# One stage of a two-layer image kernel put under a list scheduler: attention, spectral filters and weight preparation in the order of a table

## The chip, the cores and the metric

The kernel runs on one core of one Trainium2 chip. The core has a matrix engine (TensorE, PE in the profile, whose weight loads are the row PEld), a vector engine (VectorE, DVE), an activation engine (ScalarE, ACT), a general engine (GpSimd, POOL), and a queue engine (SyncE, SP) that here does nothing but issue DMAs. Each engine runs its own instructions strictly in the order in which they were written, and waits on semaphores for the others. The metric is the device time of the whole kernel in microseconds.

## The reference

The input is a batch of 16 images of 128 channels and 32 x 32 pixels, all in float32. Two "metaformer" layers are applied; each adds a token mixer and then a second mixer to the image.

```python
# layer 0: linear attention on channels, then a spectral filter over the pixels
x = x + conv0(ln_c(x))        # group norm, q/k/v, softmax(q), softmax(k), context = k v, out = context q, w_out
t = to_tokens(x)
t = t + ffn0(ln_t(t))         # sum over 16 filters: causal long convolution, then a 128x128 matrix each; 3 short taps
# layer 1: two 3x3 convolutions with a residual, then a mixture of 64 experts
x = x + conv1(ln_c(x))
t = to_tokens(x)
t = t + ffn1(ln_t(t))         # 8 best pixels per expert are gathered, gelu(x w1) w2, added back
```

`ln_c` and `ln_t` normalize each pixel over its 128 channels. The long convolution runs over 1024 channel vectors in a transform of the pixels: a sample is multiplied with cosine and sine tables (by "classes" of every eighth pixel), the spectrum is multiplied with the transform of the filters, and the result is turned back.

## The kernel before, in words

**Stages.** The kernel works through the batch in four stages, one after the other. (1) Attention of each sample, its second normalization, the three short taps, and its transform into a spectrum that is written to DRAM (lines 221 to 774). In the same stage the filters are transformed ("filters", lines 649 to 690), their matrices are mixed from four sets (into the tile `mst`, 16 steps), and the convolution weights and the inverse tables of layer 1 are prepared ("prepare", lines 692 to 735, on POOL). (2) The spectra are multiplied with the filters (lines 777 to 921). (3) Inverse transform, layer-1 convolutions and gating, sample by sample. (4) The experts and the final sum. The change touches stage 1 alone.

**One sample in stage 1** is the class `Attention`, with a method per step; a step issues one or a few instructions on one engine. In the order of the data: `tokens` (PE transposes the image by blocks of 128 pixels into a PSUM tile `big`), `moments` (DVE, four BATCH_NORM_STATS2 on that tile, line 135) and `tokens_copy` (ACT, the same tile to SBUF, line 376); `variance`, `root`, `scales` (line 127 to 129 and 390), `norm` (ACT, eight instructions, line 144); `spread`, `group`, `group_var`, `group_root`, `group_scale`; `channels` and `channels_copy` (back to channels first, line 424); `k`, `q` (PE, lines 451 and 433); maxima, exponents and sums on DVE and ACT; `k_scale` (POOL, line 476); `q_tokens`, `q_copy`, `context` (PE, line 499), `fold`, `fold2`, `out` (PE, line 534), `out_add` (DVE, line 539). Then the second half: `input` (PE, line 157), `moments2` (DVE, line 135), `input_copy` (ACT, line 550, the same PSUM tile), `scales2`, `norm2`; `even` and `odd` (PE, line 571), whose results pass ACT, DVE (`even_sums`, line 254; `odd_sums`) and POOL (`even_turns`, lines 287 to 293; `odd_turns` 1 to 4, lines 295 to 309) and go out to DRAM (`vd`, line 628); `taps_in`, `taps_copy`, `taps` (PE, line 639), `taps_add` (DVE, line 646) and a store of the image (`xd`, line 647).

**The order around the change.** PE, DVE, ACT and POOL are pinned to the order in which the program issues the steps; SP is not pinned in stage 1. The order before is a fixed period written by hand: a tuple `period` (line 742) names each step once with a distance `d`, and the loop runs it for `p` from -6 to 15 and calls each step for sample `p + d` (lines 760 to 771). So up to seven samples are in work, each step once per round; one step of the filters and one of the preparation is called per round. The first round that has a sample in all steps comes after six rounds, and the last six rounds run without new samples. `keep` (line 159) puts matmuls with no use between the steps at four places, from the table `idle` (line 354).

**Loads.** Two images are loaded ahead, then the tables `wf` and `phi` (1 MB each, lines 737 and 739); every `tokens` step loads the image two samples on (line 368). A step of the filters loads 512 KB of `mi` (line 683), and its use follows in the next round.

**The planner** `planned` (line 1783) is already in the kernel and orders stage 3. It takes a table (name, engine, microseconds, due date, what the step waits for, which tiles it opens and which it closes), a number of buffers for each tile, and a period. It keeps a clock for each engine and picks, among the steps that can start within 0.25 us of the earliest, the one with the smallest due date (due + sample x period):

```python
    hop, window, never = 0.09, 0.25, 1e18
    late = dict(PE=0.165, DVE=0.083, ACT=0.096, POOL=0.04, SP=2.0)
...
        soon = min(starts.values()) + window
        k = min((k for k, t in starts.items() if t <= soon), key=lambda k: (ops[k][2], starts[k]))
```

A step marked `DVEs`, and every POOL step, also takes a shared resource called "port", so that the two kinds are not planned at the same time. `late` is what passes from the end of a step to the moment when its result can be used; `SP=2.0` with 1.28 us for the transfer makes 3.28 us for a 512 KB load. The order that comes out is what the engines follow; the planner's clock is not kept at run time.

Of the kernel before, what the change touches and what calls it, by code (L numbers as in the profile page):

```python
# [69 lines left out]
def metaformer_kernel(ctx: ExitStack, tc: tile.TileContext, io: dict, out: bass.AP):  # L70
# [106 lines left out]
    with ExitStack() as l0:  # L177
# [43 lines left out]
        with ExitStack() as a0:  # L221
            aconst = a0.enter_context(tc.tile_pool(name="aconst", bufs=1))
            setup = a0.enter_context(tc.tile_pool(name="setup", bufs=2))
            work = a0.enter_context(tc.tile_pool(name="awork", bufs=2))


            spool = a0.enter_context(tc.tile_pool(name="spool", bufs=2))
            xpool = a0.enter_context(tc.tile_pool(name="xpool", bufs=8))
            ppool = a0.enter_context(tc.tile_pool(name="ppool", bufs=1))
            ps = a0.enter_context(tc.tile_pool(name="aps", bufs=2, space=PSUM))  # L230
# [120 lines left out]
            def small(shape, name):  # L351
                return work.tile(shape, F32, name=name, tag=name, bufs=5)

            idle = {("tokens", 1): 5, ("filters", 0): 4, ("channels", 0): 1, ("k", 1): 2}

            class Attention:
# [10 lines left out]
                def tokens(self):  # L367
                    if self.b + 2 < B:
                        load(self.b + 2)
# [4 lines left out]
                def tokens_copy(self):  # L374
                    self.tok = work.tile([P, NT, C], F32, name="tok", tag="tok", bufs=3)
                    nc.scalar.copy(self.tok, self.pt)
# [171 lines left out]
                def input_copy(self):  # L548
                    self.ub = work.tile([P, NT, C], F32, name="ub", tag="ub")
                    nc.scalar.copy(self.ub, self.pt)  # L550
# [74 lines left out]
                def odd_turns4(self):  # L625
                    butterflies(self.ao, self.xf, 1, self.sd)
                    for cs in (slice(0, 1), slice(1, NCH)) if self.b + 1 == B else (slice(NCH),):
# [21 lines left out]
            def filters():  # L649

                wfm = setup.tile([P, NQ // 2, 2 * P], F32, name="wfm", tag="mi")
                nc.vector.tensor_scalar(wfm, wf[:, 1::2, :], -1.0, None, ALU.mult)

                def values(q, dst):
                    for sgn in range(2):
                        w = wfm[:, q // 2, :] if sgn and q % 2 else wf[:, q, :]
# [4 lines left out]
                yield  # L661
                xf = spectrum_tile()
                for parity in range(2):
                    pe = class_values(parity, values)
                    t = class_copy(pe, 1)
                    ts = class_copy(pe, ROT) if parity else t
                    ab = class_sums(parity, pe, t)
                    class_differences(parity, ab, pe, ts)
                    yield
                    for part in range(2):  # L670
                        butterflies(ab, xf, parity, part)
                    if parity:
# [1263 lines left out]
```

## Time and profile before

| what | value |
|---|---|
| median of three runs | 1228.67 us (1227.26 to 1231.8) |
| the profiled execution | 1229.05 us, of which its span is 1227.0 us |
| mean granted TensorE clock | 0.988 |
| PE busy over the span | 94% |
| DVE, ACT, POOL busy | 76%, 59%, 49% |
| stage 1 | from the start to about 384 us (first matmul of stage 2 at 384.08) |
| first multiplication with the spectra | 397.91 us |

The chain of work that ended last says which engine's work the end of the kernel waited for, piece by piece. A row of a timeline gives start, length, engine, line and tile, and in brackets how long the engine had been idle before it and what released it. A busy PE is an overlapping count of pipelined matmuls: the time from one matmul group's start to the next is the better measure of its length. A window row gives the busy time of PE, PEld, DVE, ACT and POOL in a stretch, with counts, then the granted clock and the DMA share and rate.

### The profile page before, as it was taken

Reading aid. Unit: us, or ns where it says so; the run is one execution under the profiler, and the core shown is the slowest. Engines: PE = TensorE matmul, PEld = TensorE weight load, DVE = VectorE, ACT = ScalarE, POOL = GpSimd, SP = SyncE. Lnnn points to the kernel's source line nnn. Section 1 sums busy time; section 2 is a strip of 40 time slices with the busy share of each in tenths; the row PEclk is TensorE's granted clock in tenths of the full one; section 3 lists DMA queues with packets and bytes.
Section 4 is the critical chain, followed back from the end, with each engine's and each line's share of the span. In section 5 each row is a group of like instructions: output and inputs, shape, how many; then the busy total and the mean of one; then the engine's idle time right before and its main releaser. Section 6 shows DMA issues by size and latency. Waiting matters only on the chain.

```text
span 1227.0 us, 34351 instructions
## 1 busy us (share of the span) xinstructions
PE 1155.2 (94%) x14364; PEld 946.8 (77%) x14364; DVE 932.7 (76%) x1956; ACT 721.2 (59%) x1414; POOL 602.2 (49%) x800
## 2 busy tenths in 40 slices
PE   6889999999999999999997999999999999998996
PEld 4677767777677899998996888888888888885453
DVE  5888888887767677777764689898888989877335
ACT  4777777776656777877760445555555555554211
POOL 2436454664568788888882433343333333230003
PEclk9999999999999999999998999999999999999998
DMA  7004435243446244344348511233233322416998
GB/s 283 24 31 158 133 99 173 87 160 124 132 142 182 81 141 139 137 139 140 125 147 282 134 52 52 87 103 120 80 121 112 103 86 70 155 35 237 357 404 341
DMA packets 91243, 175.14 MB, mean 143 GB/s; under 512 B 5968, under 2 KB 42064, under 8 KB 90448
## 3 DMA queue, kind: packets, MB, share of 16 engines
q1 hardware_dynamic: 90448, 170.46, 41.1%
q0 software_dynamic: 640, 2.49, 0.6%
q8 instruction: 113, 1.85, 0.6%
q14 instruction: 42, 0.34, 0.1%
HBM read 110.28 MB, written 62.65 MB: 141 GB/s over the span
## 4 chain that ended last, share of the span: by engine, by line
PE 52%; DVE 22%; issue 10%; ACT 5%; DMA 5%; POOL 5%; SPq 0%; POOLq 0%; DVEq 0%; ACTq 0%
PE pcv L1013 10%; PE py L841 8%; PE pg L817 8%; PE big L639 6%; DVE bst L135 4%; PE big L172 3%; PE big L152 3%; PE big L571 3%; PE big L451 2%; PE big L534 2%; PE big L433 2%; DVE abss L1256 1%; DVE xp L1278 1%; DVE xp L1140 1%; POOL v L808 1%
## 5 line engine op out<-in xcount | busy, mean ns | idle before, releaser
L1013 PE MATMUL pcv<-v,cw 128*128 128x256 f32 x1152 | 258.2, 380 | 1.6 <-POOL v L1203 1.6
L1013 PEld LDWEIGHTS pcv<-v,cw 128*128 128x128 f32 x1152 | 214.7, 190 | 34.7 <-issue 4.9
L828 DVE COPY g<-pg 128x512 f32<-128x512 f32 x196 | 127.6, 682 | 67.9 <-PE pg L817 67.9
L830 ACT COPY g<-pg 128x512 f32<-128x512 f32 x316 | 161.1, 606 | 28.7 <-PE pg L817 27.9
L817 PE MATMUL pg<-ph,mst 32*128 32x128 f32 x4096 | 138.9, 278 | 1.4 <-DVE x L646 0.9
L817 PEld LDWEIGHTS pg<-ph,mst 32*128 32x128 f32 x4096 | 125.9, 187 | 15.6 <-DVE g L828 8.3
L841 PE MATMUL py<-g,v 128*32 128x128 f32 x4096 | 126.0, 276 | 1.9 <-POOL v L809 1.6
L841 PEld LDWEIGHTS py<-g,v 128*32 128x32 f32 x4096 | 109.2, 110 | 9.7 <-POOL v L809 2.1
L144 ACT ACTIVATE tok<-tok,sts 128x128 f32<-128x128 f32 x256 | 101.9, 480 | 16.9 <-DVE sts L1090 13.6
L135 DVE BATCH_NORM_STATS2 bst<-big 128x6 f32<-128x256 f32 x252 | 89.6, 416 | 19.9 <-PE big L152 10.7
L808 POOL TENSOR_TENSOR v<-xc 128x256 f32<-128x256 f32 x128 | 98.0, 790 | 9.9 <-DMA xc<-vd 9.2
L639 PE MATMUL big<-u,mu 128*128 128x128 f32 (+4 forms) x384 | 86.0, 380 | 0.0
L1203 POOL TENSOR_TENSOR v<-abss 128x256 f32<-128x256 f32 x64 | 49.1, 787 | 68.2 <-DVE abss L1199 56.8
L287 POOL TENSOR_TENSOR xf<-ab 128x256 f32<-128x256 f32 x34 | 24.8, 728 | 112.6 <-DVE ab L254 112.5
L1222 POOL TENSOR_TENSOR yo<-abss 128x256 f32<-128x256 f32 x32 | 23.5, 734 | 107.5 <-DVE abss L1218 107.5
L639 PEld LDWEIGHTS big<-u,mu 128*128 128x128 f32 x384 | 56.7, 191 | 18.0 <-issue 15.4
L571 PE MATMUL big<-wf,ub 128*128 128x256 f32 x256 | 63.5, 392 | 0.2
L809 POOL TENSOR_SCALAR v<-v 128x256 f32<-128x256 f32 x64 | 55.0, 860 | 5.6
L476 POOL TENSOR_TENSOR ke<-ke,ks 128x1024 f32<-128x1024 f32 x16 | 30.6, 1913 | 54.9 <-DVE qs L484 43.2
L144 ACT ACTIVATE tt<-tt,sts 128x128 f32<-128x128 f32 x120 | 47.8, 481 | 13.9 <-DVE sts L1090 13.9
L571 PEld LDWEIGHTS big<-wf,ub 128*128 128x128 f32 x256 | 47.0, 193 | 9.1 <-ACT xn L424 3.0
L915 ACT COPY yt<-py 128x512 f32<-128x512 f32 x60 | 35.1, 585 | 31.2 <-ACT g L830 17.6
(277 smaller groups left out, 2479.8 us busy)
## 6 DMA issues: line engine op xcount, KB each, us to landing
we<-in_weight SPq DMA_DIRECT2D x32, 1024.0 KB, 9.1
xc<-vd SPq DMA_DIRECT2D x64, 256.0 KB, 3.0
yd<-ys SPq DMA_DIRECT2D x32, 512.0 KB, 3.6
vd<-xf SPq DMA_DIRECT2D x15, 1024.0 KB, 5.1
y<-yd SPq DMA_DIRECT2D x15, 896.0 KB, 6.1
x<-in_x SPq DMA_DIRECT2D x16, 512.0 KB, 5.5
mi<-in_M_phi SPq DMA_DIRECT2D x16, 512.0 KB, 4.7
xd<-x SPq DMA_DIRECT2D x16, 512.0 KB, 6.2
```

What stands on the lines that cost most here:

```text
L135: nc.vector.bn_stats(bst[:, j : j + 2, :].rearrange("p j s -> p (j s)"), src[:, j : j + 2, :].rearrange("p j c -> p c j"),)
L144: nc.scalar.activation(dst[:, j, :], src[:, j, :], AF.Identity, bias=nm[:, j : j + 1], scale=r[:, j : j + 1],)
L571: nc.tensor.matmul(dst, self.ub[:, q, :], wf[:, q, :], start=True, stop=True)
L639: nc.tensor.matmul(self.pa[:, a:hi], mu[:, NF - 1 - si, tap, :], self.u[:, a - tap : hi - tap], start=(tap == 0), stop=(tap == KU - 1),)
L808: nc.gpsimd.tensor_tensor(vv[:, x, 1:, bs], e, o, op)
L809: nc.gpsimd.tensor_scalar(v[:, :, 0, bs], v[:, :, 2, bs], -1.0, None, ALU.mult)
L817: nc.tensor.matmul(pg[r][:, i], mst[rs, 4 * q + i, :], ph[rs, c, :], start=True, stop=True,)
L828: nc.vector.tensor_copy(dst, src)
L830: nc.scalar.copy(dst, src)
L841: nc.tensor.matmul(py[rows, x, kl, :], v[:, (x * NM + m) * JL + jl, 1 - ri : 3 - ri, :] .rearrange("p k b -> p (k b)"), g[:, ((x * 2 + ri) ...
L1013: nc.tensor.matmul(pc[:, i], wt[:, dy, k, :], v[:, k, dy * WT : dy * WT + HT], start=(dy == 0), stop=(dy == 2),)
L1203: nc.gpsimd.tensor_tensor(v[:, k, WT : WT + HT], self.ab[:, 0], self.ab[:, 1], op)
```

## The change

**Order.** The tuple `period` is replaced by a table in the planner's form, with one row per step of a sample, and rows `f_...` for the filters and `p_...` for the preparation, which exist once. `planned` is called with a period of 520.01, and the loop runs its order. The generator `filters` becomes a class `Filters` with a method per step. Some yields of `prepare` move, so that a step is shorter.

**Loads.** The load of an image is no longer part of `tokens`. Eight images are loaded ahead, interleaved with `wf` and `phi`; the other eight are steps of the table, which need one of eight buffers, freed by the store of an earlier image. The write of a spectrum is a step (`spec`) of its own, and `mi` loads (`f_ld0` to `f_ld15`) and uses (`f_m0` to `f_m15`) are separate steps. A load of `prepare` is issued in a step of 0.02 us (`p_0`, `p_9`, `p_18`, `p_22`), and its first use is the step after.

**Copies.** `tokens_copy` and `input_copy` become two instructions of half a tile, which is one PSUM bank each; the table lets them start 0.7 us before the end of the statistics.

**Pools.** The pools of stage 1 get `reuse_waits="tile"`, as those of stage 3 have. The small tiles get 7 buffers for 5. The useless matmuls stand at other places: 12 calls as before.

```diff
-            setup = a0.enter_context(tc.tile_pool(name="setup", bufs=2))
-            work = a0.enter_context(tc.tile_pool(name="awork", bufs=2))
+            setup = a0.enter_context(tc.tile_pool(name="setup", bufs=2, reuse_waits="tile"))
+            work = a0.enter_context(tc.tile_pool(name="awork", bufs=2, reuse_waits="tile"))
...
-                return work.tile(shape, F32, name=name, tag=name, bufs=5)
+                return work.tile(shape, F32, name=name, tag=name, bufs=7)
-            idle = {("tokens", 1): 5, ("filters", 0): 4, ("channels", 0): 1, ("k", 1): 2}
+            idle = {("begin", 0): 4, ("tokens", 1): 2, ("tokens", 2): 2, ("group", 0): 2, ("channels", 0): 2}
...
                 def tokens(self):
-                    if self.b + 2 < B:
-                        load(self.b + 2)
...
-                    nc.scalar.copy(self.tok, self.pt)
+                    for h in range(2):
+                        js = slice(h * NT // 2, (h + 1) * NT // 2)
+                        nc.scalar.copy(self.tok[:, js], self.pt[:, js])
...
-                    nc.scalar.copy(self.ub, self.pt)
+                    for h in range(2):
+                        js = slice(h * NT // 2, (h + 1) * NT // 2)
+                        nc.scalar.copy(self.ub[:, js], self.pt[:, js])
...
                     butterflies(self.ao, self.xf, 1, self.sd)
+
+                def spec(self):
                     for cs in (slice(0, 1), slice(1, NCH)) if self.b + 1 == B else (slice(NCH),):
...
+            class Filters:
+                def fetch(self, k):
+                    m, i = divmod(k, NF)
+                    self.mi = getattr(self, "mi", {})
+                    self.mi[k] = setup.tile([P, MB, C], F32, name="mi", tag="mi")
+                    nc.sync.dma_start(self.mi[k], io["M_phi"][i, :, m * MB : (m + 1) * MB, :])
+
+                def mix(self, k):
+                    m, i = divmod(k, NF)
+                    es, mi = slice(m * MB, (m + 1) * MB), self.mi.pop(k)
...
+            for b in range(2, 4):
+                load(b)
             nc.sync.dma_start(wf, io["wf"])
+            for b in range(4, 6):
+                load(b)
             phi = spool.tile([P, NQ, 2, P], F32, name="phi", tag="xf")
             nc.sync.dma_start(phi, io["phi"])
+            for b in range(6, 8):
+                load(b)
-            period = (
-                ("q_max", 3), ("out_add", 1), ("tokens", 6), ("moments", 6), ("context", 2),
...
+            table = (
+                ("load", "SP", 1.28, 2153.3, "", "x", ""),
+                ("tokens", "PE", 0.88, 4110.1, "load", "big:t tok", ""),
+                ("moments", "DVE", 1.337, -1802.8, "tokens~.6", "", "big:t"),
+                ("tokens_copy", "ACT", 1.034, 110.7, "tokens moments~.7", "", "big:t"),
...
+                ("scales", "DVE", 0.747, -1588.3, "variance root", "", ""),
...
+                ("k_scale", "POOL", 1.87, -1214.9, "k_recip", "", ""),
...
+                ("input_copy", "ACT", 1.034, 2302.1, "input moments2~.7", "ub", "big:i"),
...
+                ("spec", "SP", 2.6, -1380.7, "odd_turns4 odd_turns2 odd_turns even_turns2", "", "xf"),
...
+                ("taps", "PE", 5.22, 6831.9, "taps_copy", "big:ta", "u"),
+                ("taps_add", "DVE", 1.147, 655, "taps input", "", "big:ta"),
+                ("store", "SP", 1.28, 6675.6, "taps_add input", "", "x"),
...
+                ("f_wfm", "DVE", 0.607, 3426.6, "", "mi:w", ""),
+                ("f_val0", "PE", 3.45, 3203.6, "f_wfm f_phi", "big:f0", ""),
...
+                ("f_ld1", "SP", 1.28, 3049.5, "f_ld0", "mi:1", ""),
+                ("f_m1", "DVEs", 1.187, 5750.1, "f_ld1 f_m0", "", "mi:1"),
...
+                ("p_9", "POOL", 0.02, 2845.1, "p_8", "", ""),
+                ("p_10", "POOL", 0.96, 2246.3, "p_9", "", ""),
...
+            )
+            buffers = dict(x=8, big=3, s=2, tok=3, xn=3, qe=2, ke=2, qt=2, cx=2, wy=2, wt=2, ub=2, et=2, er=1, ab0=2, ab1=2, xf=2, sd=2, u=2, mi=2)
+            START = {
...
+                "f_wfm": 14.5, "f_val0": 20.0, "f_ld0": 30.0, "p_0": 25.0,
+            }
...
+            order = planned(
+                table, buffers, B, 520.01, lambda b, name: b > 0 and name[:2] in ("f_", "p_"),
+                lambda b, name: START.get((b, name), START.get(name, 0.0)),
+            )
+            samples, setting, preparing = {}, Filters(), prepare()
             with tc.manual_schedule(engines=PINNED):
-                for p in range(-reach, B):
-                    next(preparing, None)
-                    for name, d in period:
-                        b = p + d
...
+                keep(ps, "s", idle["begin", 0])
+                for b, name in order:
+                    kind, _, rest = name.partition("_")
...
+                    elif kind == "p":
+                        next(preparing, None)
+                    elif name == "load":
+                        if b >= 8:
+                            load(b)
+                    elif name != "store":
...
+                        getattr(samples[b], "q_" if name == "q" else name)()
+                    keep(ps, "s", idle.get((name, b), 0))
```

## The prediction

> **What bounds the kernel now.** The change is confined to stage 1 (start to 384.08 us), so I read that stage first, by windows: one while the pipeline of samples fills, six steady rounds, and, since the same planner already orders stage 3, a steady part of stage 3. Columns: window, length, busy PE, PEld, DVE, ACT, POOL, clock, DMA share, GB/s.
>
> ```profile
> 60.00:80.00 20.00, 17.25 (x152) 13.76 (x151) 18.48 (x53) 15.39 (x32) 4.04 (x2) 0.91 0.06 21
> 125.18:253.14 127.96, 123.90 (x853) 94.80 (x853) 106.27 (x260) 95.47 (x199) 66.51 (x104) 1.00 0.41 130
> 700.00:1060.00 360.00, 348.97 (x2221) 307.32 (x2219) 320.08 (x641) 193.87 (x369) 139.44 (x183) 1.00 0.29 93
> ```
>
> In the steady part PE is busy 123.90 of 127.96 us: 20.65 us of work in a round of 21.33. That is the floor for a sample; DVE (17.7 us a round), ACT (15.9) and POOL (11.1) lie under it. While the pipeline fills, DVE is nearly full (18.48 of 20) and PE is not. Next, who makes PE wait in a steady round: PE's timeline, and the entry of line 550.
>
> ```profile
> 186.60 1.89 PE L571 MATMUL big<-wf,ub 128*128 128x256 f32 x8
> 189.16 1.09 PE L172 MATMUL big<-ident,ub 128*128 128x128 f32 x8 [0.66 <-ACT ub L550]
> ...
>   DVE bst L135: 33.3, 15
> ...
>   PE big L172: 9.9, 12
> ```
>
> There is one stall a round, 0.66 us: `taps_in` waits for the copy of line 550, and that copy for the statistics of line 135 on the same tile. Over the stage it costs PE 9.9 us: 2.3 in the first two rounds, 7.6 later. Third, the fill: DVE's and ACT's timelines (two of DVE's rows, ACT's root of sample 0 ahead of them), then DVE's first work on `k`.
>
> ```profile
> 12.30 0.21 ACT L122 ACTIVATE sts<-sts 128x8 f32<-128x8 f32 x1
> ...
> 20.43 0.69 DVE L254 TENSOR_TENSOR ab<-big,et 128x512 f32<-128x512 f32 x1 [3.05 <-ACT et L245]
> 21.63 0.31 DVE L127 TENSOR_TENSOR sts<-sts 128x8 f32<-128x8 f32 x1
> ...
> 31.31 1.22 DVE L460 TENSOR_REDUCE ks<-big 128x32 f32<-128x1024 f32 x1 [2.31 <-PE big L451]
> ```
>
> Sample 0 has its root at 12.51, but its scales start at 21.63: ahead of them in DVE's order stand the filters' sums (254), which wait for the filters' matmuls, and those for `phi`, landed at 16. Last, the end of the stage on PE.
>
> ```profile
> 363.66 1.13 PE L157 MATMUL big<-ident,x 128*128 128x128 f32 x8 [1.47 <-DVE x L539]
> ...
> 384.08 0.48 PE L817 MATMUL pg<-ph,mst 32*128 32x128 f32 x2
> 385.47 12.11 PE L817 MATMUL pg<-ph,mst 32*128 32x128 f32 x318 [0.90 <-DVE x L646]
> 397.91 0.43 PE L841 MATMUL py<-g,v 128*32 128x128 f32 x8 [0.33 <-POOL v L808]
> ```
>
> From the last sample's `input` to the first multiplication pass 34 us, of which PE idles few: stage 2's generation (12.1) covers the spectrum's way through DRAM.
>
> **The change part by part.** All sums are made against the profiled execution, 1229.05 us (span 1227.0), which lies 0.4 above the median of the runs.
>
> **Fill, start.** No filter step stands ahead of sample 0 any more: `f_val0` may not be planned before 20.0. I put the scales of sample 0 at 13.5 instead of 21.63, an estimate: 12.51, plus 1.0 for a wait on `wf` (`f_wfm` is planned at 14.5, and `wf` now lands behind two more images) or on the tap matrices: **-8.1**. In the old order half of the filters' matmuls (16.08 to 19.77) ran in that hole; they now take PE's time elsewhere: **+3.7**. Two images ahead of `wf` and two ahead of `phi` are 2.1 MB; at the 324 GB/s of the first 20 us `phi` lands 6.5 us later, at 22.4. The filters' result is needed at 384, so this costs nothing; without that cover it would be 6.5. SP's queue carries these loads earlier and the first `raw` and `mi` loads later, also covered.
>
> **Fill, 29 to 104 us.** PE's waits there add up to 8.3 us (1.21, 0.40, 0.46, 0.64, 0.61, 2.71, 0.66, 1.62), 1.9 more go to useless matmuls at 42.43 and 1.9 to the clock of 0.91: 12.1. A step that is ready no longer waits for its place in a round, but DVE stays nearly full here. Between 0 and 12.1 I take half: **-6.0**. The useless matmuls, 12 calls before and after, stand in holes; moved, they cost nothing unless no hole is left, and then 12 x 0.89 = 10.7 (five calls took 4.46 us at 10.83).
>
> **Steady rounds.** The bank-wise copies let the first half of line 550 start after half of the statistics, so they shorten the chain behind the 7.6 us by about 0.7 a round, more than the 0.66 stall. What comes next is the question. The nearest row is stage 3, under the same planner: its PE waits in that window were
>
> ```profile
> PE big L172 <- DVE xp L1140: 6.6, 7, 1.8
> PE big L152 <- DVE xp L1278: 3.3, 6, 0.9
> PE big L152 <- DVE rs L1347: 1.1, 5, 0.2
> ```
>
> 11.0 of 360 us, 3.1%, at a DVE load of 89%. Here DVE is at 17.7 of 20.65, 86%, and ACT at 77%. Between 0 and 3.1% I take 1.5% of 256 us (12 rounds) = 3.8 that remain: **-3.8** net. The halves themselves cost ACT 2 x 0.58 (line 245's copy of the same shape) - 1.01 = 0.15 each, 4.8 us in 32 copies, under ACT's 23% of idle time; without that cover 4.8.
>
> **Pools by tile.** Stage 1 shows no such waits. The gain is bounded by what PE's weight loads waited for a reused tile (line 571 for ACT line 424: 3.0 us), the loss by one semaphore instruction (51 ns on PE's queue at line 841) for each of 160 tiles: 8. In stage 3, with such pools, these hide in the queue, so I take 0.
>
> **Deviation from the plan.** Two things run longer than the table says. (a) The small DVE steps. The groups' means for `scales` are 175 + 371 + 280 + 339 = 1165 ns against 0.747; `scales2` 1033 against 0.747; `group_scale` 871 against 0.647: 0.93 us a sample, 15 in all. The Trainium skill speaks against the table here: *SBUF — State Buffer*, "Who interferes with whom", says that a DVE instruction with two SBUF inputs contends with a reading GpSimd instruction for a port pair, and that the loser blocks fully. The trace agrees: line 128 takes 0.17 us alone and up to 1.06. The table gives these steps no port. By the rule with the worst partner (`k_scale`, 1.91 us, once in each of three chains) it would be 5.7 us a sample, 92 in all; I take the row, whose means contain the real encounters and already lie in the 17.7. So DVE has 2.95 us a round to absorb it. (b) Loads. A load of `mi` took this from issue to landing:
>
> ```profile
> L683 SPq DMA_DIRECT2D mi<-in_M_phi x16: 328/333/626, 25.9 to 353.1; - x16
> ...
> DMA to landing us min/median/max: 3.8/4.7/6.3
> ```
>
> The planner allows 3.28; before, a whole round passed between load and use, with no wait at line 688. If every mix stood right behind its load, DVE would wait 16 x 1.42 = 22.7 us, with the PE steps behind it on hold. On POOL, three loads (`p_9`, `p_18`, `p_22`; the first is issued early, SP being unpinned) may be followed at once by their use: 4.7 + 2 x 4.2 = 13.1, with `k_scale` and the turns queued behind, and `context` on PE waiting for `k_scale`. But mixes have late due dates and DVE leaves room for about two a round, so a buffer is mostly refilled long before. Of 35.8 + 15 us I let **+3** reach PE.
>
> **End.** `taps(14)` and `taps(15)` covered the last spectrum before. PE's other waits there (1.47, 0.39, 0.30) may go; the same chain of `input`, halves, turns, write and fetch remains. `spec` is issued at its own early due date; one step late would cost what stands ahead of it in SP's queue, a store of 512 KB. Between +5 and -3.7 (those waits and POOL's 1.5 at line 732) I take **0**. An image load waits for a store of eight samples earlier, as before (SP waited 26.6 us for it, with spectra and `mi` queued behind); planned behind the store, it holds SP no longer than before: 0.
>
> Sum: -8.1 + 3.7 - 6.0 - 3.8 + 3.0 = -11.2, hence **1217.9 us**.
>
> **The rivals.** *The stall only moves.* PE waits for another step as in stage 3 (3.1%: no steady gain) and DVE, full in the fill, gives back no part of the 12.1: -4.4, 1224.7. For: DVE at 86 and 89%; against: the stall has one cause, which the halves address. *Everything comes in.* Both fill parts whole with the filters as filler (-8.1 - 12.1), 7.6 in the rounds, -2.2 at the end, +4 for the deviation: -26, 1203. For: PE has work of other samples at hand; against: the 18.48. *Engines stand behind their loads* (slower). The price is the 35.8 us above on a gain of 14.2 without the deviation; it decides from 40% reaching PE on. At 60%: 1229.05 - 14.2 + 21.5 = 1236.4. For: the table has use after load with 3.28 or 0.06 us between; against: greedy gaps come seldom enough to let loads land.
>
> **How the numbers follow.** Forecast 0.47 (own range 1211 to 1224), stall moves 0.20, everything 0.13, loads 0.20. A change of less than 0.5% (6.1 us) can't be told from none: 1222.5 to 1234.8. Faster: forecast 0.45, everything 0.13, stall moves 0.07: 0.65. Same: 0.02, stall moves 0.11, loads 0.04: 0.17. Slower: 0.18. The range 1203 to 1238 leaves about 0.1 beyond each end.
>
> **What would show it.** Right: DVE's first line-127 work before 15 us and `k` of sample 0 near 21; rounds near 20.9 us; no row of `taps_in` waiting for line 550; first matmul of line 817 near 373. Wrong: idle time on DVE ahead of the mixes or on POOL ahead of lines 704 and 732 released by a DMA, and rounds above 21.3; or a gap between the last generation and the first multiplication of more than 5 us.

## The result

The changed kernel takes 1236.69 us (median of 20 runs, 1228.39 to 1241.64), the kernel before 1230.47 in the same session (20 runs, 1226.64 to 1234.48). The ratio is **1.0053**, 95% interval 1.0038 to 1.0068: slower by 0.5%, where the prediction said 1217.9 and faster. The profiled execution has a span of 1233.6 us against 1227.0, at nearly the same granted clock (0.989 and 0.988), so the 6.6 us between the spans stand for the 6.2 between the medians.

Five marks in the two traces, and the ends of the spans, tell where the time went (us from the start):

| mark | before | after | difference |
|---|---|---|---|
| taps of sample 0 begin | 87.38 | 91.69 | +4.3 |
| first matmul of the generation | 384.08 | 379.51 | -4.6 |
| first multiplication with the spectra | 397.91 | 398.17 | +0.3 |
| end of the last multiplication (end of stage 2) | 643.99 | 655.34 | +11.4 |
| first matmul with `tmat` in stage 3 | 674.43 | 683.08 | +8.7 |
| end of the span | 1227.0 | 1233.6 | +6.6 |

So the fill lost 4.3 us, the rounds gained 8.9, the hand-over to stage 2 lost 4.8, and **stage 2, in which no line was edited, lost 11.1**: it takes 257.2 us from the first to the last multiplication instead of 246.1. The later stages give 4.8 back. A second execution of the changed kernel (e5 below) has these marks at 91.22, 377.57, 396.18 and 653.92 us: single marks differ by up to 2 us between executions, the length of stage 2 by 0.5.

Line numbers of the changed kernel differ: 571 is 573 now, 550 is 552, 639 is 643, 817 and 841 (generation, multiplication) are 987 and 1011, 808 and 809 (POOL's turns) are 978 and 979, 870 and 871 (DVE's combines) are 1040 and 1041.

**The fill after.** PE's timeline, then DVE's (start, length, engine, line, tile; in brackets the idle time before it and its releaser).

```profile
9.66 5.35 PE L165 MATMUL wm<-ident 128*128 128x512 f32 x8 [2.71 <-DVE srow L349]
14.85 1.36 PE L152 MATMUL big<-ident,x 128*128 128x128 f32 x11
...
18.98 0.17 DVE L127 TENSOR_TENSOR sts<-sts 128x8 f32<-128x8 f32 x1 [0.24 <-ACT sts L122]
33.39 1.23 DVE L460 TENSOR_REDUCE ks<-big 128x32 f32<-128x1024 f32 x1 [1.50 <-PE big L451]
```

Four calls of useless matmuls now stand ahead of sample 0 and wait 2.71 us for DVE. Sample 0's tokens start at 14.85 us (before at 7.53). Its scales still come 2.7 us earlier than before (18.98 for 21.63), but DVE's first work on `k` is 2.1 us later (33.39 for 31.31).

**The rounds after.** Windows: length, busy PE, PEld, DVE, ACT, POOL, clock, DMA share, GB/s. Then three rows of one round: ACT's copy of line 552, DVE's statistics of line 135, PE's `taps_in` (line 172).

```profile
60.00:80.00 20.00, 17.71 (x139) 12.85 (x137) 17.10 (x41) 14.71 (x33) 15.85 (x13) 0.91 0.17 52
223.11:303.95 80.84, 80.84 (x569) 63.47 (x568) 65.35 (x169) 65.03 (x141) 38.55 (x64) 1.00 0.29 92
```

```profile
260.32 1.07 ACT L552 COPY ub<-big 128x512 f32<-128x512 f32 x2 [1.18 <-DVE bst L135]
...
258.81 1.42 DVE L135 BATCH_NORM_STATS2 bst<-big 128x6 f32<-128x256 f32 x4 [0.26 <-PE big L157]
...
250.39 1.07 PE L172 MATMUL big<-ident,ub 128*128 128x128 f32 x8
```

Four rounds take 80.84 us, 20.21 each (before 21.33), and the trace shows no idle time of PE in them: `taps_in` stands at 250.39 with no wait, since its copy was made some 10 us earlier (the row of line 552, one round of 20.21 us before). The first window says more of the fill: between 60 and 80 us POOL is busy 15.85 us, for 4.04 before. And note the rows of ACT and DVE: the first half of the copy starts at 260.32, after all four statistics (258.81 + 1.42), not after two.

**The end of the stage after.** PE, then POOL, then SP's queue; in the second fence SP's queue of the kernel before.

```profile
380.89 12.11 PE L987 MATMUL pg<-ph,mst 32*128 32x128 f32 x318 [0.90 <-DVE x L650]
398.17 0.66 PE L1011 MATMUL py<-g,v 128*32 128x128 f32 x8 [5.16 <-POOL v L978]
...
380.58 0.46 POOL L309 TENSOR_TENSOR xf<-sd 128x128 f32<-128x128 f32 x1
390.41 1.43 POOL L978 TENSOR_TENSOR v<-xc 128x256 f32<-128x256 f32 x2 [9.38 <-PE pg L987]
...
381.06 0.80 SPq L632 DMA_DIRECT2D vd<-xf  x2
381.95 2.44 SPq L651 DMA_DIRECT2D xd<-x  x1
384.48 12.34 SPq L963 DMA_DIRECT2D xc<-vd  x7
```

```profile
380.43 6.07 SPq L793 DMA_DIRECT2D xc<-vd  x3
386.68 0.80 SPq L628 DMA_DIRECT2D vd<-xf  x2
```

Before, three of the four first fetches of spectra (samples that were long done) were issued ahead of the last spectrum's write; after, all stand behind it. POOL idles 9.38 us, turns all four quarters in a row, and PE waits 5.16 us for it. (POOL's wait is put down to PE here, but it turns what the fetches bring, and these were issued only from 384.48 us on.)

**Stage 2.** What PE's weight loads waited for between 420 and 620 us (total, times, longest), after and then before; "issue" is idle time for which the profile shows no releaser.

```profile
PEld pg L987 <- issue: 7.8, 27, 0.9
PEld pg L987 <- DVE g L998: 6.3, 32, 0.2
```

```profile
PEld pg L817 <- DVE g L828: 6.7, 34, 0.2
PEld pg L817 <- issue: 4.4, 20, 0.4
```

The idle time without a releaser has grown by 3.4 us in these 200. That is a mark of what happens, and not the whole of the 11.1 us.

### The profile page after: what moved, and what is told of

It is laid out like the page before. It is cut to its first block, busy times and chain, and to the rows that moved or that the text cites. A ratio compares the mean times of both kernels' runs of the same rounds, so it can differ in the third digit from the quotient of the medians.

```text
span 1233.6 us, 34451 instructions
## 1 busy us (share of the span) xinstructions
PE 1159.0 (94%) x14364; PEld 947.9 (77%) x14364; DVE 948.9 (77%) x1956; ACT 726.6 (59%) x1446; POOL 606.4 (49%) x800
## 4 chain that ended last, share of the span: by engine, by line
PE 51%; DVE 27%; issue 11%; ACT 6%; DMA 3%; POOL 1%; SPq 0%; POOLq 0%; DVEq 0%; ACTq 0%
PE pg L987 11%; PE py L1011 10%; PE pcv L1183 10%; DVE bst L135 4%; PE big L573 4%; PE big L152 3%; PE big L643 3%; PE big L172 3%; DVE abss L1426 1%; DVE xp L1448 1%; PE big L534 1%; DVE xp L1310 1%; DVE sts L128 1%; ACT tt L144 1%; PE big L433 1%
## 5 line engine op out<-in xcount | busy, mean ns | idle before, releaser
L987 PE MATMUL pg<-ph,mst 32*128 32x128 f32 x4096 | 145.1, 281 | 4.5 <-issue 2.9
L987 PEld LDWEIGHTS pg<-ph,mst 32*128 32x128 f32 x4096 | 130.2, 188 | 20.5 <-issue 11.0
```

The lines of the kernel that those rows point to most:

```text
L987: nc.tensor.matmul(pg[r][:, i], mst[rs, 4 * q + i, :], ph[rs, c, :], start=True, stop=True,)
```

## The experiments

Each edit is shown against the kernel that the first line names; times are medians, ratios are to the kernel before in the same session.

**1. The fetch order and the number of small buffers.** In both kernels SP orders itself in stage 1; theory A in the expectations below says that the order of the fetches changes with the place of the `xc` tiles in memory. The runs change the number of buffers alone; the way by which it acts is argued.

The first edit (e1) is made in the changed kernel, the second (e2) in the kernel before.

```diff
- return work.tile(shape, F32, name=name, tag=name, bufs=7)
+ return work.tile(shape, F32, name=name, tag=name, bufs=5)
```

```diff
- return work.tile(shape, F32, name=name, tag=name, bufs=5)
+ return work.tile(shape, F32, name=name, tag=name, bufs=7)
```

> The changed kernel with five buffers for the small statistics tiles, as before the change, instead of seven; nothing else is edited. Theory A (buffer count sets the memory of the stage 2 tiles, and so the place of the first spectrum fetches in SP's order): three of the first four fetches of spectra stand far ahead, and the first multiplication comes about 14 us after the first generation instead of 18.7, so 4.8 us less at that point. A1: the stretched stage 2 (196.6 us for 8 x 6 multiplication groups against 190.2 before) is a consequence of that late start, so it goes as well: 8 more, about 1223.5 us. A2: the stretch is separate, about 1232 us. Rival B (the new order itself makes POOL's first turns late): no change, 1236 to 1238 us.

> The kernel before, with seven buffers for the small statistics tiles instead of five; nothing else is edited. Theory A: the first fetches of spectra move behind the last spectrum write and wait for TensorE, the gap from the first generation to the first multiplication grows from 13.8 to about 18.7 us: 1235 us if stage 2 is not touched (A2), 1241 to 1244 us if stage 2 stretches with it (A1). Rival B (buffer count is harmless): 1230.5 us, within 2.

e1: 1227.97 us, 0.9995 (0.9974 to 1.0017). First generation to first multiplication falls from 18.66 to 14.17 us. e2: 1236.50, 1.0061 (1.0037 to 1.0086); the gap grows from 13.83 to 19.95, with the same row as in the changed kernel:

```profile
402.25 0.66 PE L841 MATMUL py<-g,v 128*32 128x128 f32 x8 [5.02 <-POOL v L808]
```

The effect of theory A holds in both directions: seven buffers instead of five in a pool that stage 2 never uses cost 4.5 to 6 us at its start. In e1 three fetches are back ahead of the last write, and in e2 all stand behind it. A1 fell as the account of the whole stretch: e2 begins to multiply later than the changed kernel (402.25 for 398.17) and still needs only 247.4 us for stage 2; e1 begins at 391.60 and takes 253.0, 4 us less than the changed kernel and still 7 more than the kernel before. Most of the stretch of stage 2 is something else.

**2. The useless matmuls ahead of sample 0** (changed kernel).

```diff
- idle = {("begin", 0): 4, ("tokens", 1): 2, ("tokens", 2): 2, ("group", 0): 2, ("channels", 0): 2}
+ idle = {("begin", 0): 0, ("tokens", 1): 2, ("tokens", 2): 2, ("group", 0): 2, ("channels", 0): 2}
```

> The changed kernel without the four idle matmuls that it puts ahead of sample 0 (they write nothing that is read). Theory: they wait for DVE and hold TensorE to 15.0 us, so the tokens of sample 0 start near 7.5 instead of 14.85 us, DVE's first statistics near 15 instead of 18.98, and stage 1 ends 3 to 4 us earlier: 1232 to 1233 us. Rival: DVE's own first work (constants of the filters) or a lower granted clock at the start sets the pace, and the taps of sample 0 stay near 91.7 us: 1236 to 1237 us.

1232.14 us, 1.0013 (0.9996 to 1.0029). The tokens start at 7.02 us and the scales of sample 0 (line 127) at 13.80, a little earlier than expected, and close to the 13.5 that the prediction had assumed. But the taps of sample 0 begin at 89.8 us, only 1.4 to 1.9 earlier than in the two traces of the changed kernel (91.2 and 91.7). As much of the gain lies in stage 2, which takes 253.6 us (257.2 and 257.7): experiment 8 shows how fewer matmuls at the start can do that. The window from 30 to 90 us, before and then e3, each with two groups of DVE's small steps (busy us, mean ns of one, idle before), shows what took the rest:

```profile
30.00:90.00 60.00, 53.23 (x390) 41.52 (x389) 50.14 (x134) 45.17 (x91) 20.72 (x24) 0.97 0.09 29
...
L128 DVE SCALAR_TENSOR_TENSOR sts<-sts 128x8 f32<-128x8 f32 x6 | 1.6, 272 | 0.2
L127 DVE TENSOR_TENSOR ga<-ga 128x1 f32<-128x1 f32 x4 | 0.6, 145 | 0.0
```

```profile
30.00:90.00 60.00, 52.12 (x397) 38.18 (x397) 56.36 (x112) 43.15 (x89) 45.72 (x50) 1.00 0.26 80
...
L127 DVE TENSOR_TENSOR ga<-ga 128x1 f32<-128x1 f32 x3 | 3.1, 1026 | 0.6 <-ACT ga L122 0.6
L128 DVE SCALAR_TENSOR_TENSOR sts<-sts 128x8 f32<-128x8 f32 x5 | 2.8, 562 | 0.2
```

DVE is busy 56.36 of 60 us (50.14 before), with fewer instructions (112 for 134), and POOL 45.72 (20.72): the list scheduler puts preparation steps on POOL into the fill. DVE's filter steps are no more than before there (1.3 us in e3, 3.2 before). What grew are its small steps. Those of 128x8 or 128x1 elements are 70 before and take 14.0 us; in e3 52 take 20.5 us. Of these, 31 overlap an instruction of POOL and take 556 ns on average, the 21 others 158. In the changed kernel it is the same: 55 take 18.5 us, 33 of them beside POOL. So the fill loses DVE's time to POOL's earlier work. That this is all that holds the taps back is not shown: no run moves the preparation out of the fill.

**3. The copies cut in two.** e4 is the kernel before with the cut, e7 the changed kernel without it. The diff shows `input_copy`; `tokens_copy` is cut likewise.

```diff
-  nc.scalar.copy(self.ub, self.pt)
+  for h in range(2):
+      js = slice(h * NT // 2, (h + 1) * NT // 2)
+      nc.scalar.copy(self.ub[:, js], self.pt[:, js])
```

> The kernel before with one part of the change alone: the token copy and the input copy are cut in two, one for each bank, in the old periodic order. Theory: the wait of the tap transposes behind the copy behind the statistics (7.6 us over the stage) goes, at no price elsewhere: the steady round falls from 21.33 to about 20.8 us, 1222 to 1225 us. Rival (the stall only moves, or the second fixed cost of a copy on ACT eats it): 1229 to 1232 us.

> The changed kernel with the token copy and the input copy whole again, one instruction over both banks. Theory A (the cut does nothing: in the changed kernel, too, the first half starts only 0.08 to 0.1 us after the fourth statistic has ended; it is the new order that moved the copy away from the taps): the steady round stays at 20.2 us, within 0.1, and the time within 1.5 us of 1236.7. Rival B (the prediction's: the cut takes the stall away): 0.5 to 0.7 us more in each of some 13 rounds, 1243 to 1246 us.

e4: 1232.38 us, 1.0015 (1.0001 to 1.0030), round 21.39 to 21.41 for 21.33, and the stall is still there:

```profile
253.55 1.09 PE L172 MATMUL big<-ident,ub 128*128 128x128 f32 x8 [0.68 <-ACT ub L554]
```

e7: 1234.26 us, 1.0040 (1.0021 to 1.0059), round 20.21 as with the cut. So **the cut does nothing for the stall**; the first half, too, waits for the fourth statistic (in e4 the copy starts at 252.42 us, 0.08 after it has ended). The stall went by the new order, which puts other work between the copy and the tap transposes. The cut has a price elsewhere, however: stage 2 takes 250.7 us in e4 (246.1 without the cut) and 251.7 in e7 (257.2 with it). Experiment 8 takes this up.

**4. The same kernel again** (e5, no edit).

> The changed kernel as it is, profiled once more, with no edit. Question: are the 257.2 us from the first multiplication to the end of the last (246.1 before, 247.4 with seven small buffers, 250.7 with the cut copies, 253.0 with five small buffers) a property of the program or of one execution? Theory P (the program's instruction order and addresses fix it): 256 to 258 us again. Theory X (it varies from one execution to the next): somewhere else between 246 and 257 us.

257.7 us in stage 2 after 257.2: theory P. On this one repetition, the pace belongs to the program.

**5. The sixteen mixes.** e6 delays their fetches in the planner's input; e9 moves mixes and fetches in the finished order.

```diff
+ START.update({f"f_ld{k}": 30.0 + 19.0 * k for k in range(16)})
```

```diff
  order = planned(
...
  )
+ moved = [(0, f"f_{t}{k}") for k in range(3, 16) for t in ("ld", "m")]
+ order = [o for o in order if o not in moved]
+ for k in range(3, 16):
+     order.insert(order.index((0, f"f_m{k - 2}")) + 1, (0, f"f_ld{k}"))
+     at = order.index((k - 1, "even_sums"))
...
+     order.insert(at, (0, f"f_m{k}"))
```

> The changed kernel with one edit: the planner may fetch the slice of M_phi of mix k no earlier than 30 + 19 k us of its plan, so that about one mix falls to each sample, as before the change, instead of all sixteen by 207 us. Theory A (the crowd of mixes on DVE costs the rounds between 133 and 223 us their speed): the ten rounds from the taps of sample 0 to those of sample 10 fall from 212.2 us to 205 to 208, since a round has 4 us of idle DVE and a mix needs 1.2; 1230 to 1233 us. Rival B (a mix costs the round 1 us or more wherever it stands, by DVE's order or by the port that it shares with POOL): 211 to 213 us for the ten rounds, 1235 to 1238 us.

> The changed kernel with mixes 3 to 15 moved in the finished order, all else left in its place: mix k directly ahead of even_sums of sample k-1, its fetch directly behind mix k-2, so one mix and one fetch of M_phi fall to each sample, as before the change. The planner does not see it, so nothing else is re-planned. Theory A (the crowd of mixes is what slows the rounds between 133 and 223 us): the taps of sample 0 to those of sample 10 take 204 to 207 us instead of 211 to 212; 1228 to 1232 us if stage 2 stays near 257 us. Rival B (a mix costs 1 us wherever it stands): 210 to 213 us, 1235 to 1238 us.

e6: **1290.79 us**, 1.0485 (1.0449 to 1.0521), which no theory had. DVE does not wait for a load of `mi`; PE waits for DVE (PE's chief waits from 90 to 370 us, and one row):

```profile
PE big L534 <- DVE wt L528: 9.3, 3, 5.7
PE big L534 <- DVE sts L127: 8.9, 2, 4.6
...
266.01 3.75 PE L534 MATMUL big<-xn,wt 128*128 128x512 f32 x4 [2.79 <-DVE sts L382]
```

The intervals between the taps of successive samples are now 36.7, 10.5, 26.0, 35.1, 9.6, 47.9 us: with other release times the scheduler gives another order of everything, two samples at a time, and its due dates may not suit that. The experiment tells nothing of the mixes. e9, which leaves the rest in place, does: 1238.91 us, 1.0073 (1.0049 to 1.0097). From the taps of sample 0 to those of sample 10 it takes 213.8 us, the changed kernel 212.3. That is rival B's number: moving the mixes gains nothing. Its reason, that a mix costs 1 us wherever it stands, is not shown by this, since the moved mixes make a hole elsewhere:

```profile
134.03 0.79 PE L515 MATMUL pw<-wout,cx 128*128 128x128 f32 x2 [3.15 <-DVE cx L506]
```

What slows the two rounds from 154 to 202 us of the changed kernel (23.36 and 24.11 us) is in part visible (2.15 us of wait for DVE's `gt`, a clock of 0.96, one `out` of another sample, 1.98 us) and else open.

**6. Edits together.** e8: five buffers, no useless matmuls at the head, and the mixes as in e6. e10: the same with the mixes as in e9.

> The changed kernel with three edits together: five small buffers instead of seven, no idle matmuls ahead of sample 0, mixes spread over the samples as in the run with that edit alone. If the three gains add (8.7 and 4.5 us as measured alone, 4 to 6 expected of the spread): 1218 to 1221 us, faster than the kernel before. Rival (an earlier and denser stage 1 is handed back in the stretch of stage 2, which took 253 us or more in every kernel with the new order): 1225 to 1229 us.

> The changed kernel with three edits: five small buffers, no idle matmuls ahead of sample 0, mixes moved in the finished order as in the run with that edit alone. Gains that add: 8.7 and 4.5 us as measured alone, 4 to 8 for the mixes: 1216 to 1221 us, faster than the kernel before by 0.8 to 1.1%. Rival (stage 2 stretches to 257 us): 1224 to 1228 us.

e8: 1278.83 us, 1.0399 (1.0357 to 1.0440), the re-planned order again, with 247.7 us in stage 2. e10: 1227.14, 0.9972 (0.9955 to 0.9989): the rival's time, though stage 2 took 250.6 us and not 257; the moved mixes gave nothing, as the run e15 below, without them, confirms (0.9953).

**7. POOL's work beside DVE's combines.** A combine (the two DVE steps of lines 1040 and 1041 that follow a multiplication) takes 0.42 us alone and 0.95 beside POOL; 37 of 64 second combines were slow in the changed kernel, 30 of 64 before. Here the turns are left out for all classes but the first, in both kernels.

```diff
  def turns(c, i):
...
+     if c:
+         vs[c] = vs[0]
+         xcs.pop((c, i))
+         return
```

> The changed kernel with the turns of stage 2 left out on POOL for every class but the first (all classes multiply with the turned spectra of the first; the fetches stay, the result is another). Theory C (what separates the stage 2 of the programs, 246 to 258 us, is how often DVE's combines run while POOL works, 0.42 us alone and 0.95 us beside it): from the first multiplication to the end of the last 238 to 247 us, and within 2 us of the same edit in the kernel before. Rival D (TensorE's own stalls without a visible wait, or the fetches, separate them): 250 us or more here.

> The kernel before with the turns of stage 2 left out on POOL for every class but the first (all classes multiply with the turned spectra of the first; the fetches stay, the result is another). Theory C (DVE's combines beside POOL's work set the pace of stage 2): 238 to 246 us from the first multiplication to the end of the last, within 2 us of the same edit in the changed kernel. Rival D: 245 to 247 us here, as with the turns, and 8 us less than the same edit in the changed kernel.

So all classes multiply with the turned spectra of the first, and the result is another. 13 slow second combines are left in each, yet stage 2 takes 253.9 us in the one and 244.1 in the other. Theory C fell: the encounters are worth 2.0 and 3.3 us, and 9.8 us of the difference stay (totals of one execution each: 1235.49 and 1224.40). With fewer of these encounters a pattern stands out. e11, PE in one step of the loop (64 matmuls of generation, 64 of multiplication):

```profile
526.41 0.93 PE L991 MATMUL pg<-ph,mst 32*128 32x128 f32 x19
527.90 1.61 PE L991 MATMUL pg<-ph,mst 32*128 32x128 f32 x45 [0.56 <-issue]
```

In e11 all twelve stalls that split a generation group between 425 and 650 us come after exactly 19 of its matmuls. In each kernel the place is its own (38 before, 27 in e7, 15 in the changed kernel, in the middle of stage 2), and in most it creeps towards the start of the group by about one matmul in 30 us. And the DMA queues, between 430 and 610 us of e11, have a row that fits:

```profile
q8 instruction: 44, 0.72, 1.5%
```

44 packets of 16.4 KB in 180 us, one each 4.1 us: one packet of instructions for each step of the loop, 128 weight loads with their matmuls. A packet's border therefore falls on nearly the same matmul of every step, and which one it is depends on the number of instructions ahead of stage 2. The packets' own times in the traces agree. In e11 all 13 stalls of weight loads over 0.25 us inside a group from 420 us on end 1.3 to 1.5 us after a packet of this queue has landed; in e13 below there are 32, from 0.27 to 1.5 us long, and all end 1.2 to 1.6 us after a landing. How long a stall was makes no difference to that, so what PE waits for comes at a fixed time behind the packet.

**8. Moving the border.** A number of tiny matmuls (N below) at the head of PE's program, where it waits for its first data.

```diff
+ zero = aconst.tile([32, 32], F32, name="zero")
+ nc.vector.memset(zero, 0.0)
+ zp = big()
+ for _ in range(N):
+     nc.tensor.matmul(zp[:32, :8], zero, zero[:, :8], start=True, stop=True)
```

e13: kernel before, N = 24. e14: changed kernel, N = 104. e15: changed kernel, five buffers and no useless matmuls at the head, N = 0. e16 and e17: e15 with N = 112 and 48. e18: kernel before, N = 56.

> The kernel before with 24 tiny matmuls (32x32 weights, 8 columns, of zeros) at the head of TensorE's program, while it waits for its first data; nothing reads them. Theory I (the pace of stage 2 depends on where in its loop the 16 KB packets of TensorE's instructions begin: 128 pairs of weight load and matmul, one step of the loop, fill one packet, and the stalls without a releaser come after 38 to 40 matmuls of a generation group before, after 13 to 19 in the changed kernel): the stalls move 24 matmuls up, to about 14, and the time from the first multiplication to the end of the last grows from 246 to 254 to 258 us; 1238 to 1242 us in all. Rival E (the pace has another cause, the place of the stall is only its mark): 245 to 248 us, 1230 us.

> The changed kernel with 104 of the same tiny matmuls at the head of TensorE's program. 104 pairs are 24 short of one packet, so by theory I the stalls move from about 14 to about 38 matmuls into the generation group, and the time from the first multiplication to the end of the last falls from 257 to 246 to 249 us; 1225 to 1230 us in all. Rival E: 256 to 258 us, 1236 us.

> The changed kernel with five small buffers and without the idle matmuls ahead of sample 0; the mixes stay crowded as the change has them. The stalls should come near 22 matmuls into the group, as in the run without the idle matmuls, so 250 to 253.5 us in stage 2. Stage 1 ends some 1.6 us earlier than with the mixes moved as well, by the rounds of that run: 1223 to 1227 us. Rival (the moved mixes did help): 1228 to 1230 us.

> The changed kernel with five small buffers, without the idle matmuls ahead of sample 0, and with 112 of the tiny matmuls at the head of TensorE's program, 16 pairs short of one packet. Theory I: stalls near 38 into the group, stage 2 at 245 to 248 us, 4 to 6 us less than with the two edits alone, 1217 to 1222 us in all, faster than the kernel before. Rival E: no gain over the two edits alone, or a loss of 1 us for the longer start.

> The changed kernel with five small buffers, without the idle matmuls ahead of sample 0, and with 48 of the tiny matmuls at the head instead of 112. Each of them shows as two matmuls in the trace, so 48 move the packets by 96 pairs, and 112 by 224, which is 96 past a whole packet: the same place in the loop, 56 to 50 into the generation group. By theory I stage 2 stays at 244 to 246 us; the head takes 5.4 us instead of 12.1 and is done near 7, so the taps of sample 0 come near 91 us instead of 94.4: 1216 to 1218 us, the fastest of all. Rival (stage 2 is not set by the place): 249 to 254 us in stage 2, 1222 us or more.

> The kernel before with 56 of the tiny matmuls at its head: 112 pairs, so the packets begin 16 matmuls later in the group, near 54 instead of 38, the place of the fastest version. By theory I stage 2 takes 244 to 246 us instead of 246 to 247; the head costs about 1 us at the start: 1229 to 1231 us. What then separates it from that version is the order of stage 1 and its start alone. Rival (any padding at the head changes the pace, whatever the place): 250 us or more in stage 2.

In the traces of e13 and e14 each tiny matmul shows as two (48 for 24), so the border moved twice as far as expected: in e13 not to 14 of the generation group but to 52 to 58 of the multiplication group, in e14 to 62 (worked out; one short stall of 0.16 us shows it there).

Places are those in the middle of stage 2.

| kernel | border: place in the step | stage 2, us | total, us | ratio (95%) |
|---|---|---|---|---|
| before | generation 38 | 246.1 | 1230.47 | |
| changed | generation 15 | 257.2 | 1236.69 | 1.0053 (1.0038 to 1.0068) |
| e13 | multiplication 55 | 267.2 | 1243.23 | 1.0113 (1.0093 to 1.0133) |
| e14 | generation 62 | 245.0 | 1227.78 | 0.9986 (0.9970 to 1.0003) |
| e15 | generation 23 | 250.0 | 1225.91 | 0.9953 (0.9937 to 0.9969) |
| e16 | generation 53 | 244.4 | 1220.52 | 0.9927 (0.9904 to 0.9949) |
| e17 | generation 52 | 244.8 | **1214.07** | **0.9878** (0.9855 to 0.9901) |
| e18 | generation 54 (worked out) | 243.4 | 1223.14 | 0.9979 (0.9961 to 0.9997) |

The stalls of e13, PE in one step and PE's waits from 420 to 620 us; then PE's weight loads in e14:

```profile
507.87 0.49 PE L846 MATMUL py<-g,v 128*32 128x128 f32 x9 [1.23 <-issue]
...
PE py L846 <- issue: 12.9, 23, 1.2
```

```profile
PEld pg L992 <- DVE g L1003: 6.9, 35, 0.2
PEld pg L992 <- issue: 2.9, 15, 0.2
```

Theory I holds: e14 alone takes 12 us out of stage 2 without touching it, e13 puts 21 in, e16 and e17 (the same remainder by another count) agree within 0.4 us, and the kernel before reaches the same pace at the same place. The tiny matmuls also bring a tile of zeros and one turn of a PSUM tile, but these are the same in e13 and e18, which differ in N alone and lie 23.8 us apart in stage 2.

The traces say as well what had moved the border. Ahead of stage 2, PE has 2332 matmuls and as many weight loads in both kernels; but a wait on a semaphore is an instruction too, and of these PE has 46 there before and 96 after. 50 more are the length of 25 pairs of a weight load and a matmul, and the border moved by 23. In e3 the four calls that are gone are eight matmuls less, and its border lies at 22 instead of 15. The cut copies account for about half: e4 (old order, with the cut) and e7 (new order, without it) both have 73, and both take nearly the same in stage 2 (250.7 and 251.7 us). The rest comes with the new order or with the pools by tile; no run tells these apart.

The border is not the whole of it. e1 has 96 such waits like the changed kernel, but five buffers, and takes 253.0 us instead of 257.2; e15 takes 250.0 and e3, the same with seven buffers, 253.6. So in the new order the two buffers also cost some 4 us inside stage 2, in a way that is not shown. Nor is it shown why one place costs more than another. In e11 the stalls come mostly four or more steps apart, as the loop's large transfers do, so a packet behind a burst of data might be the late one; that is argued only.

e17 beats the kernel before by 1.2% and, through the ratios, the changed kernel by 1.7%.

## Why the prediction was wrong

By the marks of the result, the sum of -11.2 missed the +6.6 of the spans like this: the fill was to give 10.4 us (-8.1 + 3.7 - 6.0) and lost 4.3; stage 2 had no term and lost 11.1; the end had 0 and lost 4.8; the rounds, with the +3 for deviations, were to give 0.8 and gave 8.9; the later stages, without a term, gave 4.8.

- **Stage 2 was given no term.** "The change is confined to stage 1" is true of the code and false of the time. The new program has 50 more waits on semaphores in PE's instructions ahead of stage 2, the border of the packets moved from matmul 38 to 15 of the group, and stage 2 lost 11.1 us; moving the border alone gave 12.2 back (e14). The prediction had priced such waits, under the pools, as 51 ns each on PE's queue, hidden there, and not as a shift of all that follows. No row of the profile of before would have given the size, though the repeated "issue" of stage 2 was in its waits.
- **Fill, start: -8.1.** The scales came at 18.98, not 13.5. "The useless matmuls, 12 calls before and after, stand in holes" failed for the four that stand ahead of sample 0: 2.71 us of wait and 5.35 us of work on the path. Without them the start is as predicted (13.80), but that is worth only 1.4 to 1.9 us at the taps of sample 0.
- **Fill, 29 to 104 us: -6.0.** Half of PE's slack was to come in. None did: the taps of sample 0 start 4.3 us later. The condition that I named, a DVE that "stays nearly full here", is what the traces show: 84% before, 94% in e3. The step that failed is under the deviations: "I take the row, whose means contain the real encounters" took the means of the old order. With POOL's preparation drawn into the fill, DVE's small steps there take 18.5 us in the changed kernel for 14.0 before, though they are fewer.
- **Steady rounds: -3.8, right sign, wrong reason.** The stall went, but not by the bank-wise copies (e4, e7). The order did it, and did more: 1.12 us a round from 223 to 304 us. Before that, two rounds are slow (23.36 and 24.11 us, in part unexplained), and from sample 0's taps to sample 10's only 3.8 us are gained; the last rounds add 5.1. Together 8.9.
- **Loads: part of +3.** DVE waited 0.8 us for `mi` in two places and no rival came of it; "engines stand behind their loads" is not why the kernel is slower. That this rival's 1236.4 lies next to the measured 1236.69 is luck.
- **End: 0, between +5 and -3.7.** Measured +4.8, near the bound, by another mechanism than the one named there: not a late `spec`, but the fetches behind it, and their order changes with two more buffers in a pool of small tiles (e1, e2). I had not asked what seven buffers do to the memory of the next stage.
- **Pools by tile: 0.** Open. No run has them alone. They may bring some of the 50 waits on semaphores that moved the border.

Measured against the kernel before with the border at a good place in both, the change as it stands is worth little (e14: 0.9986, with a head 3 us longer; e18: 0.9979). With five buffers, without the useless matmuls at the head and with the border at a good place, the new order is worth 0.7 to 1.0% (e17 against e18: 0.7 by the medians, 0.8 by the spans, 1.0 by the ratios); the first generation comes 10.0 us earlier (374.65 for 384.69). That the forecast's 0.9% lies near this is luck: the terms that made it up, the fill above all, did not come true, and the rounds gave far more than theirs.

## What to carry to other kernels

An edit that leaves a stage's code alone can still change it, through what it inherits: the place of its tiles in memory, the order of a queue that orders itself, and the number of instructions ahead of it, waits on semaphores included. Before a difference of 1% is put down to a schedule, look in the untouched stages for a stall that recurs at the same instruction, and shift the program by a few harmless instructions. And a list scheduler with due dates fitted to one plan is no knob: new release times for one kind of step cost 4.8%.

## What the runs showed of the hardware

- PE's instruction packets (16.4 KB each by the queue's row) can be late even in straight code: 12.9 us of stalls in 200 us in e13, up to 1.23 us each, all of them ending 1.2 to 1.6 us after a packet has landed. The Trainium skill, *Runtime: NRT & Kernel Launch*, "Instruction fetch mechanics", says that instructions are refilled in 16 KiB blocks and that the cost of crossing a border is mostly hidden. The size agrees; the cost, 243 to 267 us for one stage by the border's place, does not.
- A tiny fp32 matmul (32x32 weights, 8 columns) appears as two matmuls in the trace, and 208 of them take 11.26 us, 54 ns each.
- A copy of one bank of a two-bank tile started only 0.1 us after the last statistic on the other bank had ended. Whether the chip or the program's waits do that is not shown.
- DVE's small steps (128x8 and 128x1 elements) took 158 ns on average when POOL was idle and 556 beside POOL's work (e3, 30 to 90 us).
- From the first matmul with `tmat` in stage 3 to the end of the span, where the code is the same in all, e13 takes 546.7 us and e15 555.0. Two executions of the changed kernel differ there by 3.5 us (550.6 and 554.1), so only a part can belong to the program. This is not explained.
